# Two message-passing layers on one core: layer two's sums on three column groups of TensorE, and a second fetcher of rows

## The chip, the core and the metric

The kernel runs on one core of a Trainium2 chip. A core has five engines with queues of their own: TensorE (PE, matrix products; its weight loads are shown as PEld), VectorE (DVE), ScalarE (ACT), GpSimd (POOL) and SyncE (SP). SP, ScalarE and POOL also issue transfers (DMAs). The metric is the time of the whole program on the device in microseconds; less is better.

## What is computed

A graph has 6250 nodes and 200,000 edges. A node has 160 features: 64 scalars and 32 vectors of three components. Each edge has a source `src`, a destination `dst` (sorted), four attributes `sh` (one scalar `e0`, one vector `e1`) and ten more, `ea`. Both layers have the same shape: gather the source's row, make a message of it with the edge's attributes, sum the messages by destination, and multiply the sums by small matrices. After each layer comes a residual and a layer norm.

```python
# layer one
m = concat(out0(ss, e0, dot(vv, e1)), out1(ss, vv, e0, e1))     # linear in the source's row
m_agg = segment_sum(m, dst)
x = layernorm(x + (x + relu(linear(m_agg))))
# layer two
w0, w1, w2, w3 = split(relu(ea @ W_fc1) @ W_fc2)                # 64, 64, 32, 32 per edge
y0, y1 = l0[src], l1[src]                                       # linear maps of x, gathered
m0 = w0 * y0 * e0;   m1 = (w1 * y0) * e1;   m2 = (w2 * e0) * y1;   m3 = w3 * dot(y1, e1)
s0..s3 = segment_sums of m0..m3 by dst
x = layernorm(x + self_linear(x) + 0.5 * linear(s0, s3, s1, s2))
```

## The kernel before

**Chunks and tiles.** The edges are cut into 391 chunks of 512. A chunk is four tiles (`J = 4`) of 128 edges, one edge in each partition. Since `dst` is sorted, all edges of a chunk fall into one window of at most 32 neighbouring nodes (or, in the 79 chunks from `HALF = 312` on, into two windows, one for each half of the partitions; there are 470 windows). `ORDER` interleaves these two kinds of chunks: eight of the first kind, then now and then four of the second.

**A chunk's way.** The 128 source rows of a tile are gathered by POOL with an indirect DMA (`gathered`, L244 to L247), from `x` in layer one and from the table `ytab`, which layer one writes, in layer two. The gathered tile `g` comes from a ring of `GRING = 8` chunks. VectorE builds a one-hot matrix of destinations in the window and multiplies it with the four attributes (`onehot`, L453 to L463): `S` has, for each of four tiles, 4 x 32 = 128 columns, 32 for each attribute. In layer two `hidden` (L465, TensorE and ScalarE) and `message` (L477, TensorE's `pw`, VectorE) make the edge's weights and from them the message `m`, two times 160 values for an edge: the first 160 go with attribute 0, the second 160 with attributes 1 to 3.

**The sums.** `matmuls` (L496) multiplies `S` with `g` (layer one) or `m` (layer two), over the four tiles of a chunk, into a PSUM tile `ab` for each window. The rows of `ab` are the 4 x 32 columns of `S`. In layer two one product has 320 columns, and of its 128 x 320 result only two parts are of use: rows 0 to 31 of the first 160 columns, and rows 32 to 127 of the second 160. `joined` (L508, ScalarE) copies the first part over the rows 0 to 31 of the second, so that one block of 128 x 160 is left. `add` (L513) transposes it in blocks of 32 x 32 on VectorE into the free end of `ab`, and adds it to `acc`, which holds the sums of all nodes. When all edges of 128 nodes are done, the parts listed in L650 to L656 project the sums, add the residual and do the norm. A `fp32` product leaves two records in the trace, each of all its columns.

**Two queues help POOL.** Of every 16 chunks SP fetches the last tile of one (place 15), and in layer one ScalarE does so for another (place 7), row by row with the row number from a register: `fetch_rows` (L380). In each of the 16 chunks ahead, the helper loads eight numbers into registers (L396) and issues eight transfers of 640 B (L400). The numbers themselves come by a transfer on SP's queue (`numbers`, L376), ordered halfway through the 16 chunks before, into one of two buffers. `place_rows` (L402) copies the 128 fetched rows into the ring on ScalarE.

**The order of work.** It is written out by hand in L657 to L669: for each step `t` every stage is issued for the chunk `t` less its lag (L649 for layer two: fetching and loading 0, one-hot and hidden 1, message 2, products 3, copy and addition 4). Each engine works through its own share of this list in order. POOL carries only the gathers.

Of the kernel before, what the change touches and what calls it, by code (L numbers as in the profile page):

```python
# [10 lines left out]
F32 = mybir.dt.float32  # L11
BF16 = mybir.dt.bfloat16
I32 = mybir.dt.int32
AF = mybir.ActivationFunctionType
# [4 lines left out]
P = 128  # L19
N = 6250  # L20
E = 200000
D = 160
M0, M1 = 64, 32
J = 4
CH = P * J
NCH = -(-E // CH)
# [12 lines left out]
W = 32  # L39
# [9 lines left out]


EVERY = 16
ROWS = P // EVERY
FOLD = 104


# [29 lines left out]

ORDER = interleaved()
POS = {c: i for i, c in enumerate(ORDER)}
# [165 lines left out]
def windowed(ctx: ExitStack, tc: tile.TileContext, x, srcs, src, rel, low, ident, iota, early, ahead, ea, sh, avec,  # L253
# [6 lines left out]
    nc = tc.nc  # L260
# [94 lines left out]
    def sums(layer, table, gp, hp):  # L355
        with ExitStack() as s:
# [5 lines left out]
            rp = s.enter_context(tc.tile_pool(name=f"r{layer}", bufs=2))  # L362
            pa = s.enter_context(tc.tile_pool(name=f"pa{layer}", bufs=3 if layer else 4, space=PSUM))
# [4 lines left out]
            G, S, SH, ET, H, M, PA, AT, RAW, NUM, ROW = ({} for _ in range(11))  # L368


            helpers = {EVERY - 1: (nc.sync, mybir.EngineType.SP)}
            if not layer:
                helpers[EVERY // 2 - 1] = (nc.scalar, mybir.EngineType.Activation)
            helped = {ORDER[i] for i in range(EVERY // 2, NCH) if i % EVERY in helpers}

            def numbers(c):  # L376
                NUM[c] = rp.tile([1, P], I32, name=f"num{POS[c] % EVERY}")
                nc.sync.dma_start(NUM[c], src[:, c, J - 1:J].rearrange("p a -> a p"))

            def fetch_rows(c):  # L380
                i = POS[c]
                for place, (queue, engine) in helpers.items():

                    k = (i - place - 1) % EVERY
                    due = i - k + EVERY - 1
                    if due >= NCH or ORDER[due] not in helped:
                        continue
                    d = ORDER[due]
                    if d not in NUM:
                        numbers(d)  # L390
                    if d not in ROW:
                        ROW[d] = rp.tile([P, D], F32, name=f"row{place}")
                    if k == EVERY // 2 and due + EVERY < NCH:
                        numbers(ORDER[due + EVERY])
                    a = k * ROWS
                    _, at = nc.values_load_multi_w_load_instructions(  # L396
                        NUM[d][0:1, a:a + ROWS], engines=[engine], min_val=0, max_val=N - 1,
                        skip_runtime_bounds_check_because="node numbers")
                    for n in range(ROWS):
                        queue.dma_start(ROW[d][a + n:a + n + 1, :], table[ds(at[n], 1), :])  # L400

            def place_rows(c):  # L402
                if c in helped:
# [92 lines left out]
            def matmuls(c):  # L496
                one = S.pop(c)
                t = M.pop(c) if layer else G[c]
                n = t.shape[2]
                h = P // len(windows(c))  # L500
                PA[c] = [pa.tile([P, n + D], F32, name="ab") for w in windows(c)]
                for j in range(J):
                    for i, ab in enumerate(PA[c]):
                        nc.tensor.matmul(ab[:, :n], one[h * i:h * i + h, j, :, :], t[h * i:h * i + h, j, :],  # L504
                                         start=(j == 0), stop=(j == J - 1), skip_group_check=True)
                del G[c]

            def joined(c):  # L508

                for ab in PA[c]:  # L510
                    nc.scalar.activation(ab[0:32, D:2 * D], ab[0:32, 0:D], AF.Copy)  # L511

            def add(c):  # L513
                for w, ab in zip(windows(c), PA.pop(c)):
                    if w % 8 == 0:
                        n = min(8, NWIN - w)
                        _, AT[w // 8] = nc.values_load_multi_w_load_instructions(
                            low[0:1, w:w + n], engines=[mybir.EngineType.DVE], min_val=0, max_val=N,
                            skip_runtime_bounds_check_because="clamped on chip")

                    n = D * (layer + 1)
                    tr = ab[:, n:].rearrange("p (b f) -> p b f", f=W)
                    blocks = ab[:, :n].rearrange("p (l b f) -> p l b f", b=5, f=32)
# [38 lines left out]
            def normed(name, b):  # L562
                r = rows(b)
                rs = np_.tile([P, 1], F32, name="rs")
                nc.vector.reciprocal(rs[:r], T.pop(("sd", b))[:r])
                o = T[name, b] = T.pop(("z", b))
                nc.vector.tensor_scalar(o[:r], o[:r], T.pop(("mv", b))[:r, 0:1], rs[:r],
                                        op0=ALU.subtract, op1=ALU.mult)
# [494 lines left out]
```

## Time and profile before

| | |
|---|---|
| median of 3 runs | 5906.23 us (5887.63 to 5917.96) |
| the profiled execution | 3964.1 us, of which the span is 3962.0 |
| mean granted clock of TensorE in it | 0.773 |
| POOL busy | 2900.8 us (73%), gathers of layer one 1428.3, of layer two 1460.6 |
| TensorE busy | 3157.5 us (80%); products `ab` of layer two 977.7, `pw` 662.3 |
| VectorE busy | 2009.5 us (51%) |
| ScalarE busy | 494.3 us (12%) |
| DMA engines | mean 75 GB/s; the 16 engines are busy 20 to 30% |
| row fetches | 3072 by SP in each layer, 2944 by ScalarE in layer one |

The profile shows one execution. Layer one fills its first 1930 us, layer two the rest. "Busy" leaves out the time that an engine spends on issuing transfers and on waiting. In the lines of groups the columns are: line, engine, operation, out<-in and count; then busy us and mean ns of one; then idle us of the engine just before, with what ended most of it. In the waits: who waited for whom, us in all, times, longest. In the timeline: start, duration, engine, line, operation, count. The profiled execution is a good deal shorter than the timed runs.

### The profile page before, as it was taken

To read this page: it belongs to the slowest core of one execution; us is meant where nothing else is said; L and a number is where in the kernel's file an instruction comes from. 1 tells how busy PE (TensorE), PEld (TensorE's weight loads), DVE (VectorE), ACT (ScalarE), POOL (GpSimd) and SP (SyncE) were. 2 spreads that over 40 slices of the span, in tenths; PEclk is the share of its full clock that TensorE was granted. 3 is DMA by queue.
4 is the path that set the end of the run, shared out by engine and by line. 5 is a ranking of instruction groups with operands and counts; after the bars stand their busy time and mean duration, and the time that the engine had idled before them with its cause. 6 is when DMAs were issued, how large, how long until landed. Compare 5 with 4: busy or idle time off the path is not lost.

```text
span 3962.0 us, 71344 instructions
## 1 busy us (share of the span) xinstructions
PE 3157.5 (80%) x12754; PEld 2196.2 (55%) x12755; DVE 2009.5 (51%) x6485; ACT 494.3 (12%) x1288; POOL 2900.8 (73%) x3062
## 2 busy tenths in 40 slices
PE   3346677777777777766799899999999999999998
PEld 3334444444554444544566566666666666666666
DVE  4223323333333334344466666666666666666666
ACT  2000000000000000001111111111111111111111
POOL 6777777777777777777677777777777777666763
PEclk7656655555556566666799999999999899898999
DMA  3322233333333333333232323233333332222321
GB/s 82 74 69 73 73 76 74 75 75 80 75 78 76 79 77 81 77 81 81 71 77 73 76 73 77 75 77 76 78 79 75 78 79 73 70 74 71 76 70 49
DMA packets 223655, 297.53 MB, mean 75 GB/s; under 512 B 77638, under 2 KB 166988, under 8 KB 223194
## 3 DMA queue, kind: packets, MB, share of 16 engines
q0 software_dynamic: 146736, 250.63, 25.6%
q1 hardware_dynamic: 63382, 35.55, 3.4%
q10 hardware_dynamic: 13076, 6.70, 0.6%
q14 instruction: 354, 2.90, 0.2%
q8 instruction: 107, 1.75, 0.2%
HBM read 280.61 MB, written 12.00 MB: 74 GB/s over the span
## 4 chain that ended last, share of the span: by engine, by line
PE 31%; issue 16%; DMA 16%; POOL 14%; SPq 13%; DVE 5%; ACTq 4%; ACT 1%; DVEq 0%; POOLq 0%
PE ab L504 15%; POOL g L247 14%; SPq L400 9%; PE pw L484 8%; DMA g<-in_x,srcs 7%; PE ph L471 4%; ACTq L400 3%; SPq L396 3%; DMA g<-ytab,srcs 3%; DMA row<-in_x 2%; DVE m L492 2%; PE ph L548 1%; DMA early<-in_ea 1%; PE bank L635 1%; ACTq L396 1%
## 5 line engine op out<-in xcount | busy, mean ns | idle before, releaser
L247 POOL DMA_INDIRECT g<-ytab,srcs x1540 | 1460.6, 948 | 541.3 <-issue 408.3
L247 POOL DMA_INDIRECT g<-in_x,srcs x1505 | 1428.3, 949 | 463.6 <-issue 401.9
L504 PE MATMUL ab<-g,S 128*128 128x160 f32 (+1 forms) x3736 | 1038.9, 463 | 552.9 <-DMA g<-in_x,srcs 300.2
L504 PEld LDWEIGHTS ab<-g,S 128*128 128x128 f32 (+1 forms) x3736 | 696.4, 278 | 902.6 <-DMA g<-in_x,srcs 498.1
L504 PE MATMUL ab<-m,S 128*128 128x320 f32 (+1 forms) x3760 | 977.7, 456 | 2.2 <-DVE acc L529 2.0
L504 PEld LDWEIGHTS ab<-m,S 128*128 128x128 f32 (+1 forms) x3760 | 632.7, 201 | 222.8 <-issue 56.0
L484 PEld LDWEIGHTS pw<-fc,h 100*128 100x128 f32 x3128 | 552.5, 203 | 252.5 <-issue 153.0
L484 PE MATMUL pw<-fc,h 100*128 100x192 f32 x3128 | 662.3, 356 | 27.0 <-DVE bank L458 16.2
L462 DVE TENSOR_TENSOR S<-bank,sh 128x384 f32<-128x384 f32 (+2 forms) x782 | 431.2, 551 | 197.2 <-PE ab L504 164.7
L487 DVE TENSOR_TENSOR m<-pw,g 128x256 f32<-128x256 f32 x782 | 328.1, 420 | 373.3 <-PE pw L484 251.0
L527 DVE STREAM_TRANSPOSE ab<-ab 128x160 f32<-128x160 f32 x470 | 169.5, 361 | 677.2 <-PE ab L504 673.1
L492 DVE TENSOR_TENSOR m<-g,pw 128x192 f32<-128x192 f32 x1564 | 474.7, 344 | 0.0
L529 DVE TENSOR_TENSOR acc<-acc,ab 128x120 f32 (+2 forms) x940 | 261.4, 278 | 210.4 <-ACT acc L585 144.0
L474 ACT ACTIVATE h<-ph 100x512 f32<-100x512 f32 x391 | 228.3, 584 | 377.4 <-PE ph L471 377.4
L511 ACT ACTIVATE ab<-ab 32x160 f32<-32x160 f32 x470 | 119.7, 264 | 1208.9 <-PE ab L504 1042.4
L458 DVE TENSOR_TENSOR bank<-ramp,rel 128x96 f32<-128x96 f32 (+2 forms) x782 | 199.7, 255 | 88.2 <-PE bank L635 86.4
L471 PE MATMUL ph<-early,fc 10*100 10x512 f32 x392 | 135.9, 707 | 77.1 <-DMA early<-in_ea 77.1
L525 DVE STREAM_TRANSPOSE ab<-ab 128x160 f32<-128x160 f32 x470 | 167.3, 356 | 20.9 <-ACT ab L511 11.8
L471 PE MATMUL ph<-w_or_et,fc 10*100 10x512 f32 x390 | 128.3, 665 | 57.2 <-DMA w_or_et<-in_ea 57.1
L622 DVE SCALAR_TENSOR_TENSOR base<-pl,a_sb,z 128x160 f32<-128x160 f32 (+1 forms) x49 | 18.8, 384 | 265.7 <-ACT y L619 260.5
L548 PE MATMUL ph<-w_or_et,acc 128*128 128x160 f32 (+1 forms) x490 | 126.7, 436 | 3.5 <-DVE acc L529 2.2
L548 PEld LDWEIGHTS ph<-w_or_et,acc 128*128 128x128 f32 (+1 forms) x490 | 118.7, 304 | 13.2 <-issue 6.7
(95 smaller groups left out, 847.8 us busy)
## 6 DMA issues: line engine op xcount, KB each, us to landing
row<-in_x SPq DMA_DIRECT2D x3072, 0.6 KB
row<-ytab SPq DMA_DIRECT2D x3072, 0.6 KB
row<-in_x ACTq DMA_DIRECT2D x2944, 0.6 KB
g<-ytab,srcs POOLq DMA_INDIRECT x1540
g<-in_x,srcs POOLq DMA_INDIRECT x1505
raw<-in_sh SPq DMA_DIRECT2D x88, 64.0 KB
early<-in_ea SPq DMA_DIRECT2D x98, 40.0 KB
xt<-in_x SPq DMA_DIRECT2D x48, 80.0 KB
```

The source lines that it names most:

```text
L247: nc.gpsimd.indirect_dma_start(out=g[:, j, :], out_offset=None, in_=table, in_offset=bass.IndirectOffsetOnAxis(ap=srcs[:, c, j:j + 1], axi ...
L400: queue.dma_start(ROW[d][a + n:a + n + 1, :], table[ds(at[n], 1), :])
L458: nc.vector.tensor_tensor(oh[:, :, :w], iota[:, None, :w].to_broadcast([P, J, w]), rel[:, c, :, None].to_broadcast([P, J, w]), op=ALU.is_e ...
L462: nc.vector.tensor_tensor(S[c][:, :, :, :w], oh[:, :, None, :w].to_broadcast([P, J, 4, w]), attr[:, :, :, None].to_broadcast([P, J, 4, w]) ...
L471: nc.tensor.matmul(ph[:, i, :], fc1[g:g + 10, :], ET[c // 4][g:g + 10, c % 4 // 2, :], start=True, stop=True)
L474: nc.scalar.activation(H[c], H["p"][:, c % 2, :].rearrange("f (p j) -> f j p", j=J), AF.Relu, scale=FC_SCALE)
L484: nc.tensor.matmul(pw[:, j, :], h[:, q + j, :], fc2, start=True, stop=True)
L487: nc.vector.tensor_tensor(mq[:, :, :, 0:64], pw[:, :, 0:128].rearrange("p j (a u) -> p j a u", a=2), y[:, :, None, 0:64].to_broadcast([P, ...
L492: nc.vector.tensor_tensor(mq[:, :, a, 64:160].rearrange("p j (d u) -> p j d u", d=3), y1, pw[:, :, None, w:w + 32].to_broadcast([P, 2, 3, ...
L504: nc.tensor.matmul(ab[:, :n], one[h * i:h * i + h, j, :, :], t[h * i:h * i + h, j, :], start=(j == 0), stop=(j == J - 1), skip_group_check ...
L529: nc.vector.tensor_tensor(v, v, tr[:, :, :width(c)], op=ALU.add)
L548: nc.tensor.matmul(po[:r], lhs, weights[:, g, :], start=(g == 0), stop=(g == 4))
```

## The change

In layer two `matmuls` now issues three products of 160 columns for each tile and window in place of one of 320: attribute 0 with the first 160 columns of `m` (PSUM partitions 0 to 31), attribute 1 with the second 160 (32 to 63), attributes 2 and 3 with the second 160 (64 to 127). Each product uses a column group of the array of its own (32, 32 and 64 columns). The results lie where `add` wants them, `joined` goes, and the tile `ab` shrinks from 480 to 320 columns.

ScalarE becomes a helper in layer two as well, at place 7 of every 32 chunks: four rows in each of 32 chunks, eleven tiles in all (POOL then has 1529 gathers in layer two, where it had 1540). In both layers and for both helpers the numbers have one buffer now in place of two, and they are ordered when the helper has read the last of the numbers before, in the last of its 16 (or 32) chunks, one chunk ahead of their use.

```diff
-            helpers = {EVERY - 1: (nc.sync, mybir.EngineType.SP)}
-            if not layer:
-                helpers[EVERY // 2 - 1] = (nc.scalar, mybir.EngineType.Activation)
-            helped = {ORDER[i] for i in range(EVERY // 2, NCH) if i % EVERY in helpers}
+            helpers = {EVERY - 1: (nc.sync, mybir.EngineType.SP, EVERY),
+                       EVERY // 2 - 1: (nc.scalar, mybir.EngineType.Activation, EVERY * (layer + 1))}
+            helped = {ORDER[i] for place, (_, _, every) in helpers.items() for i in range(every - 1, NCH)
+                      if i % every == place}
 
-            def numbers(c):
-                NUM[c] = rp.tile([1, P], I32, name=f"num{POS[c] % EVERY}")
+            def numbers(c, place):
+                NUM[c] = rp.tile([1, P], I32, name=f"num{place}", bufs=1)
                 nc.sync.dma_start(NUM[c], src[:, c, J - 1:J].rearrange("p a -> a p"))
...
-                    if k == EVERY // 2 and due + EVERY < NCH:
-                        numbers(ORDER[due + EVERY])
-                    a = k * ROWS
+                    n = P // every
+                    a = k * n
                     _, at = nc.values_load_multi_w_load_instructions(
-                        NUM[d][0:1, a:a + ROWS], engines=[engine], min_val=0, max_val=N - 1,
+                        NUM[d][0:1, a:a + n], engines=[engine], min_val=0, max_val=N - 1,
                         skip_runtime_bounds_check_because="node numbers")
-                    for n in range(ROWS):
-                        queue.dma_start(ROW[d][a + n:a + n + 1, :], table[ds(at[n], 1), :])
+                    if k == every - 1 and due + every < NCH:
+                        numbers(ORDER[due + every], place)
+                    for m in range(n):
+                        queue.dma_start(ROW[d][a + m:a + m + 1, :], table[ds(at[m], 1), :])
...
             def matmuls(c):
                 one = S.pop(c)
                 t = M.pop(c) if layer else G[c]
-                n = t.shape[2]
                 h = P // len(windows(c))
-                PA[c] = [pa.tile([P, n + D], F32, name="ab") for w in windows(c)]
+
+                sides = ((0, 1, 0), (1, 2, D), (2, 4, D)) if layer else ((0, 4, 0),)
+                PA[c] = [pa.tile([P, 2 * D], F32, name="ab") for w in windows(c)]
                 for j in range(J):
-                    for i, ab in enumerate(PA[c]):
-                        nc.tensor.matmul(ab[:, :n], one[h * i:h * i + h, j, :, :], t[h * i:h * i + h, j, :],
-                                         start=(j == 0), stop=(j == J - 1), skip_group_check=True)
+                    for a, b, n in sides:
+                        for i, ab in enumerate(PA[c]):
+                            p = slice(h * i, h * i + h)
+                            nc.tensor.matmul(ab[W * a:W * b, :D], one[p, j, a:b, :], t[p, j, n:n + D],
+                                             start=(j == 0), stop=(j == J - 1), skip_group_check=True)
                 del G[c]
-
-            def joined(c):
-
-                for ab in PA[c]:
-                    nc.scalar.activation(ab[0:32, D:2 * D], ab[0:32, 0:D], AF.Copy)
...
-                    if layer:
-                        nc.vector.transpose(tr, blocks[:, 1])
-                    else:
-                        nc.vector.transpose(tr, blocks[:, 0])
+                    tr = ab[:, D:].rearrange("p (b f) -> p b f", f=W)
+                    nc.vector.transpose(tr, ab[:, :D].rearrange("p (b f) -> p b f", f=32))
...
-                stages = [(fetch_rows, 0), (load, 0), (place_rows, 1), (joined, 4), (onehot, 1), (hidden, 1), (add, 4), (message, 2), (matmuls, 3)]
+                stages = [(fetch_rows, 0), (load, 0), (place_rows, 1), (onehot, 1), (hidden, 1), (add, 4), (message, 2), (matmuls, 3)]
```

More of the change, by code (lines that the diff above doesn't have):

```diff
@@ L51 @@
 EVERY = 16
-ROWS = P // EVERY
 FOLD = 104
@@ L381, in fetch_rows @@
                 i = POS[c]
-                for place, (queue, engine) in helpers.items():
-                    k = (i - place - 1) % EVERY
-                    due = i - k + EVERY - 1
+                for place, (queue, engine, every) in helpers.items():
+                    k = (i - place - 1) % every
+                    due = i - k + every - 1
                     if due >= NCH or ORDER[due] not in helped:
@@ L389, in fetch_rows @@
                     if d not in NUM:
-                        numbers(d)
+                        numbers(d, place)
                     if d not in ROW:
                         ROW[d] = rp.tile([P, D], F32, name=f"row{place}")
-                    if k == EVERY // 2 and due + EVERY < NCH:
-                        numbers(ORDER[due + EVERY])
-                    a = k * ROWS
+                    n = P // every
+                    a = k * n
                     _, at = nc.values_load_multi_w_load_instructions(
-                        NUM[d][0:1, a:a + ROWS], engines=[engine], min_val=0, max_val=N - 1,
+                        NUM[d][0:1, a:a + n], engines=[engine], min_val=0, max_val=N - 1,
                         skip_runtime_bounds_check_because="node numbers")
-                    for n in range(ROWS):
-                        queue.dma_start(ROW[d][a + n:a + n + 1, :], table[ds(at[n], 1), :])
+                    if k == every - 1 and due + every < NCH:
+                        numbers(ORDER[due + every], place)
+                    for m in range(n):
+                        queue.dma_start(ROW[d][a + m:a + m + 1, :], table[ds(at[m], 1), :])
             def place_rows(c):
@@ L519, in add @@
                             skip_runtime_bounds_check_because="clamped on chip")
-                    n = D * (layer + 1)
-                    tr = ab[:, n:].rearrange("p (b f) -> p b f", f=W)
-                    blocks = ab[:, :n].rearrange("p (l b f) -> p l b f", b=5, f=32)
-                    if layer:
-                        nc.vector.transpose(tr, blocks[:, 1])
-                    else:
-                        nc.vector.transpose(tr, blocks[:, 0])
+                    tr = ab[:, D:].rearrange("p (b f) -> p b f", f=W)
+                    nc.vector.transpose(tr, ab[:, :D].rearrange("p (b f) -> p b f", f=32))
                     v = acc[:, :, ds(AT[w // 8][w % 8], width(c))]
```

## The prediction

> **What bounds the kernel now.** I read the page's row of slices first, then the groups of each layer by window, the stretches, the waits of the last third of layer two, and last the timeline of TensorE and POOL. First the page:
>
> ```profile
> PE   3346677777777777766799899999999999999998
> POOL 6777777777777777777677777777777777666763
> PEclk7656655555556566666799999999999899898999
> ```
>
> Slices are 99 us. POOL holds one share in both layers, while TensorE is busiest, at nearly full clock, in layer two (from slice 20). What POOL's share means is told by its groups, first in 1932 to 3200 us, then in 3200 to 3900:
>
> ```profile
> L247 POOL DMA_INDIRECT g<-ytab,srcs x1012 | 959.5, 948 | 328.9 <-issue 270.2 <-DMA btab<-base 20.6 <-DVE m L492 14.0
> L247 POOL DMA_INDIRECT g<-ytab,srcs x518 | 491.6, 949 | 208.4 <-issue 135.4 <-DVE bank L458 31.6 <-DVE m L492 24.9
> ```
>
> The first has 1012 gathers in 1268 us, 1.253 us each: 0.948 of work and 0.30 of issue, with nothing between. The second has 518 in 700 us, 1.351 each. At 1.254 they would take 650, so 50 us went to waits for VectorE, that is, for a buffer that compute had not emptied. Layer one (1516 gathers in 1906 us) has 5 us of such waits. The waits of 3200 to 3900 say whom compute waits for:
>
> ```profile
> POOL g L247 <- DVE bank L458: 31.6, 25, 3.7
> PE ph L471 <- DMA w_or_et<-in_ea: 31.2, 12, 3.5
> PE ph L471 <- DMA early<-in_ea: 27.8, 10, 4.2
> ```
>
> TensorE stands 59 us for the edge features that SP's queue brings late, and after such a wait its clock is low for some microseconds. Now TensorE's timeline in a good stretch of layer two (start, duration, name, count):
>
> ```profile
> 3027.28 0.49 PE L484 MATMUL pw<-fc,h 100*128 100x192 f32 x2
> 3027.61 2.32 PE L504 MATMUL ab<-m,S 128*128 128x320 f32 x8
> 3029.86 1.10 PE L471 MATMUL ph<-w_or_et,fc 10*100 10x512 f32 x4
> 3030.89 1.57 PE L484 MATMUL pw<-fc,h 100*128 100x192 f32 x8
> 3032.30 2.32 PE L504 MATMUL ab<-m,S 128*128 128x320 f32 x8
> 3034.45 1.47 PE L484 MATMUL pw<-fc,h 100*128 100x192 f32 x8
> 3035.75 0.43 PE L504 MATMUL ab<-m,S 128*128 128x320 f32 x1
> ```
>
> From 3027.61 to 3035.75 are two chunks: 4.07 us each. The projections add 0.17 (bank group: 490 records over 391 chunks, some 1.4 us per ten). So TensorE wants 4.24 us a chunk at full clock, and POOL 1540 x 1.254 / 391 = 4.94. **POOL is the bound, TensorE is close behind**, and takes over where its clock falls. Last, the ends: POOL's last gather is at 3912.4, the span ends at 3962.0, and TensorE is busy 41 of these 50 us with the chunks it is behind.
>
> The profiled execution took 3964.1 us (span 3962.0 and 2.1 around it). **The three timed runs have a median of 5906.2, which is 1942 more, and no row says where.** TensorE at half clock all through layer two would not do: 2 x 4.24 x 391 = 3316, with layer one's 1932 and the tail 5300. So I carry a difference over twice, as it stands (an added constant) and times 1.49 (everything slower alike), and place the forecast between, nearer the first.
>
> **The change, part by part.** (1) *The product of 320 columns becomes three of 160, on 32, 32 and 64 columns of the array.* A product stands as two records (1248 products, 2496 records). In the timeline a record of 192 columns takes (3035.75 - 3034.45) / 8 = 0.163 us, one of 320 (3034.45 - 3032.30) / 8 = 0.269, which makes 0.83 ns a column and 0.135 us for 160. A chunk has 8 records now, 2.15 us, and 24 after. If the three groups run at once: 8 x 0.135 = 1.08. If one after the other: 24 x 0.135 = 3.24. The trace has no product on neighbouring column groups. It has them on row groups, in the chunks of two windows:
>
> ```profile
> 3017.58 0.49 PE L484 MATMUL pw<-fc,h 100*128 100x192 f32 x2
> 3018.00 2.42 PE L504 MATMUL ab<-m,S 64*128 64x320 f32 x16
> ```
>
> Sixteen records in the time of eight: two row groups run side by side in full. The Trainium skill ("TensorE: Matmul & The Clock Gate", section "Part 3: Packing small matmuls — row/col tiling") gives 2.38 times for three column groups, by which I estimate 8 x 3 x 0.135 / 2.38 = 1.36 us. I take that: 0.79 saved a chunk, 4.24 becomes 3.45. For two-window chunks the same, since the halves still pair (24 pairs).
>
> A rule speaks against it: "TensorEngine Tiling (Array Packing)", section "Tiling Modes", says that a change of the tiling mode, and not merely of the tile, drains the array, and 32 and 64 columns are two modes. The nearest rows are in layer one, at half clock:
>
> ```profile
> 400.46 0.42 PE L598 MATMUL xp<-ident,z 128*128 128x128 f32 x1
> 400.68 0.42 PE L599 MATMUL xp<-ident,z 128*32 128x128 f32 x1
> 400.89 0.74 PE L504 MATMUL ab<-g,S 128*128 128x160 f32 x2
> ```
>
> 128 columns, then 32, then 128 again: 0.22 and 0.21 us apart, no step at the change. A change of row groups does show one: from two pw records to ab it is 0.42 at 3017.58 against 0.33 at 3027.28. By the row the change of columns costs 0. By the rule it costs 2 x 4 x 0.09 = 0.72 a chunk, and the wide group no longer overlaps the narrow ones (4 passes of 0.135 for each j, 2.16 in all, no gain): 4.24 + 0.73 = 4.97, just over POOL's 4.94, some +30 us and more stalls. I go by the row.
>
> A second cost is the number of instructions: 48 loads and products a chunk in place of 16, and 96 where there are two windows. The densest run of them in the trace is ten pairs in 1.64 us at half clock, 0.16 a pair, and that with 79 to 104 columns to load. At 0.16 a pair a chunk would take 3.9, at nothing 1.08. I put no price on it, since the pairs there are held by the columns loaded, and keep it for the range.
>
> (2) *The copy of 32 rows on ScalarE goes* (470 x 0.264 = 120 us of ScalarE, 0.46 of delay before VectorE's transpose where there are two). It lies beside POOL's gathers: nothing, now and after.
>
> (3) *ScalarE fetches one tile in 32 chunks of layer two*: eleven tiles, so 11 gathers x 1.254 = 13.8 us off POOL, on the bound. It pays with 11 x 128 row fetches. One costs 0.30 of its queue in layer one (0.235 and two register steps), four of them 1.2 a chunk, and the load of the numbers up to 0.82. ScalarE is busy 17% of layer two, so 2 us of 4.94 lie in its idle time. Queued behind them on ScalarE are the relu of the next chunk and the square root of the norm, for which TensorE and VectorE wait. TensorE has most of a chunk of slack once (1) holds, and the ring of eight tiles some 20 us. Nothing, then; were that slack gone, 2 us on some chunks.
>
> (4) *The numbers are ordered one chunk ahead, in one buffer, in place of eight chunks and two.* SP must wait until the helper has read the old ones (11 times in layer two, 23 in layer one, ScalarE's place), and behind that stand SP's edge features and rows. The helper then reads them one chunk later. SP is tied to VectorE anyway at each block's output (its wait there is 178 us in 36 times in layer two). Between 0 and 34 x 4.2 us, where 4.2 is the longest wait on a late transfer above. Layer one's POOL passes ScalarE's waits of 466 us for rows with 5 us lost, so I take 0.
>
> **Sum.** Gathers -13.8. Stalls of POOL: 51 becomes some 10, -41 (a less busy TensorE has a lower clock, as layer one's 0.55 to 0.65 shows, so not to nothing). Tail: seven chunks left at 0.79 less, and a smaller lag to begin with: -15 (layer one ends 21.5 after its last gather, so -28 at most, -6 at least). Together -70 of 3964, 3894. On the timed median: 5906 - 70 = 5836, or 5906 - 104 = 5802; forecast **5828**. What stays is 1529 gathers: the large saving on TensorE lies off the path.
>
> **The rivals.** *Column groups run one after the other (ends slower).* Place: every ab product of layer two. 4.24 + 1.09 = 5.33 us a chunk, 391 x 5.33 = 2084 against the 1980 between first and last gather, and with TensorE the bound its waits for edge features (126 us in layer two) count in part: +170 on the profile, 6076 to 6160, say 6100. It decides once a chunk's sums exceed 2.85 (4.94 - 4.24 + 2.15). For: no row shows neighbouring column groups at once; the drain rule and the floor per pair end here too. Against: row groups do it in full. *The gain is eaten.* Drain or pair floor leaves TensorE where it was; only the gathers go: 5906 - 14 to -25, 5885. *The timed runs are held by TensorE*, not by POOL, and 0.79 a chunk counts at half clock: 5906 - 391 x 1.6 = 5280. For: the missing 1942 us. Against: the 5300 above. *The queues bite*: (3) and (4) cost more than the gathers give, at most 34 x 4.2 less 14: between 5935 and 6035, say 5990.
>
> **How the numbers follow.** Forecast case 0.46, its own range 5775 to 5870. One after the other 0.27, gain eaten 0.13, timed runs held by TensorE 0.08, queues 0.06. What a measurement of this kernel can tell from no change is 0.5%, 30 us. Faster 0.46 + 0.08 = 0.54; same 0.13; slower 0.33. Range: at the low end the case at 5280 is left out (0.08) and the scaled gain kept, 5710; at the high end one after the other with the factor 1.49 (170 becomes 253) is kept, 6190, and full drains on top are left out.
>
> **What would show it.** Right: ab records 128x160 on three groups starting within some 10 ns, ab under 1.6 us a chunk, POOL at 75.6% busy in all stretches of layer two, TensorE's clock below 0.9, the last gather near 3860, tail near 35. Wrong: ab over 2.85 us a chunk, starts 0.135 apart, POOL under 73% from the start of layer two; or waits of SP and ScalarE at the numbers of several microseconds with edge features later than now.

## The result, and the profile after

| | before | changed |
|---|---|---|
| median, 4 runs each | 5912.09 us (5887.63 to 5927.44) | 6173.54 us (6151.01 to 6200.72) |
| ratio | | 1.0448, 95% interval 1.0388 to 1.0508 |
| the profiled execution | 3964.1 us | 6151.0 us, span 6149.1 |

The change costs 261 us, 4.5%, where a gain of 78 was forecast. To read the numbers one thing must be known: the chips of these runs are of two kinds, on one of which (chip A below) the kernel before takes 3957 us, and on the others (chips B) 5827 to 5917, so that every ratio here is against runs of before on the same chip. One chip of the runs below is of the first kind, four are of the second. The profile shown of before is like that of chip A (e1 below); the timed runs of the table, and the profile of the changed kernel, are like those of chips B.

The page of the changed kernel, its row of slices (154 us each) and the gathers of the two layers, with the products of layer two between them:

```profile
PE   2222232343333343444578888888888888888988
...
POOL 4444444544444444544444444444444544444442
PEclk7555565665565666666678887888878888888889
...
L246 POOL DMA_INDIRECT g<-ytab,srcs x1529 | 1451.0, 949 | 1646.8 <-DVE bank L458 679.8
L246 POOL DMA_INDIRECT g<-in_x,srcs x1505 | 1427.3, 948 | 1538.6 <-PE ab L507 830.4
L507 PE MATMUL ab<-m,S 128*32 128x160 f32 (+2 forms) x11280 | 1599.9, 354 | 260.6 <-issue 223.6
```

A gather still takes 0.949 us, and TensorE's clock in layer two is 0.7 to 0.8 where it was 0.9. POOL, busy 73% before, is at 47%. Most of that is the kind of chip and not the change: a kernel in which only the order of the numbers is new (e6 below, on a chip B) has POOL at 49% and a mean clock of 0.81 in layer two, where the changed kernel has 0.82. POOL has 1.5 to 1.6 ms of idle time in each layer, and the largest part of it is put down to TensorE in layer one and to VectorE in layer two, that is, to tiles that compute has not emptied. In layer two the wait for VectorE's `bank` (the comparison that makes the one-hot matrix) is 680 us, against 37 in layer two of before and 469 in e6, whose two lines are these:

```profile
POOL g L247 <- DVE bank L458: 37.4, 44, 3.7
```

```profile
POOL g L247 <- DVE bank L461: 468.7, 123, 12.8
```

The sums of layer two take 1600 us in place of the 978 of before. The waits of the changed kernel from 3050 us on, and those of SP's queue, name what compute waits for:

```profile
POOL g L246 <- DVE bank L458: 679.8, 165, 12.7
...
ACT h L474 <- DMA row<-ytab: 403.2, 110, 17.8
...
ACT g L405 <- DMA row<-ytab: 111.0, 20, 11.4
```

```profile
SPq L400 <- DMA row<-ytab: 254.8, 187, 9.9
```

ScalarE, which should have fetched rows in idle time, holds its relu `h` for 403 us until rows land, and SP's queue stands 255 us at its own row fetches, waiting for rows that are under way. Neither wait was in the profile before, and e6 has 28 us of SP's and none of `h` for rows. (Waits on chips B are to be read with care: many semaphore updates are not in their traces, 2895 of VectorE's 4297 and 2994 of TensorE's 3657 being recorded here against 4773 of 4876 and 3574 of 3632 in e1, so that a wait can be put down to the wrong engine.) Last, TensorE's timeline in a good stretch of layer two:

```profile
5248.61 1.63 PE L628 MATMUL bank<-wc,acc 128*128 128x160 f32 x10
5250.16 1.10 PE L471 MATMUL ph<-w_or_et,fc 10*100 10x512 f32 x4
5251.20 1.57 PE L484 MATMUL pw<-fc,h 100*128 100x192 f32 x8
5252.70 3.32 PE L507 MATMUL ab<-m,S 128*32 128x160 f32 x24
5255.94 1.57 PE L484 MATMUL pw<-fc,h 100*128 100x192 f32 x8
5257.44 1.27 PE L507 MATMUL ab<-m,S 128*32 128x160 f32 x9
5259.11 0.31 PE L507 MATMUL ab<-m,S 128*32 128x160 f32 x1 [0.39 <-issue]
5260.52 1.64 PE L507 MATMUL ab<-m,S 128*64 128x160 f32 x12 [1.10 <-issue]
```

The 24 records of a chunk take 5255.94 - 5252.70 = 3.24 us, while `pw` beside them takes 1.57 as it does at 3030.89 of before, so at the same clock. 3.24 is the price forecast for groups one after the other, not the 1.36 hoped for. And in the last three rows TensorE stops between two products and waits for nothing that the profile shows; the profile of before has no such pause.

### The profile page after: what moved, and what is told of

It reads as the page before. It is cut to its first block, busy times and chain, and to the rows that moved or that the text cites. A ratio compares the mean times of both kernels' runs of the same rounds, so it can differ in the third digit from the quotient of the medians.

```text
span 6149.1 us, 90380 instructions
## 1 busy us (share of the span) xinstructions
PE 3697.8 (60%) x20274; PEld 2235.2 (36%) x20275; DVE 2001.5 (33%) x6485; ACT 395.2 (6%) x829; POOL 2890.3 (47%) x3051
## 5 line engine op out<-in xcount | busy, mean ns | idle before, releaser
L507 PE MATMUL ab<-m,S 128*32 128x160 f32 (+2 forms) x11280 | 1599.9, 354 | 260.6 <-issue 223.6
L507 PE MATMUL ab<-g,S 128*128 128x160 f32 (+1 forms) x3736 | 769.1, 415 | 1156.7 <-ACT g L405 725.3
L507 PEld LDWEIGHTS ab<-m,S 128*32 128x32 f32 (+2 forms) x11280 | 612.1, 126 | 1226.4 <-issue 1212.0
L484 PE MATMUL pw<-fc,h 100*128 100x192 f32 x3128 | 741.5, 388 | 31.4 <-issue 25.6
L484 PEld LDWEIGHTS pw<-fc,h 100*128 100x128 f32 x3128 | 604.5, 223 | 277.0 <-issue 224.1
L605 PE MATMUL pl<-w_or_et,xT 128*128 128x320 f32 (+1 forms) x98 | 65.7, 771 | 472.9 <-ACT xT L598 345.6
L471 PE MATMUL ph<-w_or_et,fc 10*100 10x512 f32 x390 | 147.5, 747 | 95.1 <-DMA w_or_et<-in_ea 93.3
L605 PEld LDWEIGHTS pl<-w_or_et,xT 128*128 128x128 f32 (+1 forms) x98 | 23.8, 298 | 485.4 <-ACT xT L598 353.4
```

The source lines that it names most:

```text
L471: nc.tensor.matmul(ph[:, i, :], fc1[g:g + 10, :], ET[c // 4][g:g + 10, c % 4 // 2, :], start=True, stop=True)
L484: nc.tensor.matmul(pw[:, j, :], h[:, q + j, :], fc2, start=True, stop=True)
L507: nc.tensor.matmul(ab[W * a:W * b, :D], one[p, j, a:b, :], t[p, j, n:n + D], start=(j == 0), stop=(j == J - 1), skip_group_check=True)
```

## The experiments

**Which kind of chip (e1, e5, e12, e16).** The two kernels themselves, unedited. The kernel before, on chip A:

> The kernel before, unchanged, for a second profile of it. The profile shown of it lasts 3964 us, its timed runs 5906. If the timed state is another way of running (SP's and ScalarE's queues in stretches of 0.7 us per instruction, as in the profile after), this profile lasts some 5900 us and shows such stretches, several hundred us of gaps over 0.3 us on SP between its row fetches, where the first one shows 123. If the first profile is the rule, it lasts 3964 again.

3946.5 us, span 3944.4, and the same profile as the one shown: layer one's gathers end at about 1907 us. So the 1942 us that no row of the first profile explained go with the place where the same program runs. Each chip was used in one stretch of time only, so whether it is the chip, its host or the hour isn't shown. The changed kernel, on three chips B:

> The changed kernel, unchanged, on the chip where the kernel before takes some 3960 us. Groups alone cost 161 us there (1.041) and helpers alone 228 us (1.058). If the two causes add up, ratio 1.09 to 1.10. If both only take the same slack (the sums are late either way), 1.06 to 1.07.

> The changed kernel once more. Where before takes 3957 us: the sums alone cost 161 us there and the fetches alone 229 us. If both act through the same slack of TensorE they don't add: 4190 to 4260; if they add, 4345. Where before takes 5840 to 5910: 1.045 times before again.

> The changed kernel once more. Where before takes 3957 us: 4190 to 4260 if its two parts act through the same slack of TensorE, 4345 if they add. Where before takes 5.84 to 5.92 ms: 1.046 times before again.

1.0466 (1.0426 to 1.0505), 1.0467 (1.0422 to 1.0511) and 1.0517 (1.0481 to 1.0553), against before at 5837, 5917 and 5827 us. The changed kernel itself never ran on a chip A.

What differs between the kinds shows in SP's queue in layer one. First before on chip A, then the changed kernel on a chip B, from about the same moment:

```profile
795.77 15.89 SPq L400 DMA_DIRECT2D row<-in_x  x32
```

```profile
795.80 17.22 SPq L400 DMA_DIRECT2D row<-in_x  x22
```

A row, with its share of the loads of numbers, costs the queue 0.50 us in the one and 0.78 in the other. Not every row is dearer: from one row to the next it is 0.41 us in the median of both runs. But in the first 8 us of the second line most of SP's instructions begin 0.70 us after the one before, or twice that, where the first line has steps of 0.06 to 0.31 between the loads; and the register instructions among them have no wait recorded. Such bursts come again and again. The sums of the pauses between two instructions (over 0.38 us each, ahead of an instruction without a recorded wait; from the trace's records, us):

| kernel | SP | ScalarE | TensorE |
|---|---|---|---|
| before, chip A (e1) | 0.5 | 0 | 0 |
| changed, the profile above | 893 | 356 | 218 |
| numbers' order only (e6) | 959 | 309 | 7 |
| fetches and order (e14) | 921 | 303 | 6 |
| three groups only (e13) | 820 | 258 | 155 |
| four equal groups (e8) | 870 | 250 | 436 |
| three products on 128 columns (e17) | 901 | 263 | 258 |
| no row fetches (e9) | 8 | 0 | 22 |
| no row fetches, four groups (e10) | 2 | 0 | 418 |

All but e1 are on chips B. The sums are low: register instructions of some 0.03 us that are recorded with 0.70 themselves come on top (863 us on SP in the changed kernel, none in e1). SP and ScalarE have the pauses with row fetches and not without them; TensorE has next to none with the products of before, and many with more products. VectorE and POOL have 1 and 0 us of them in the changed kernel.

**The three groups alone (e2 on chip A, e13 and e18 on chips B).** The edit of `matmuls`, `joined` and `add`; helpers and numbers as before.

```diff
-                    for i, ab in enumerate(PA[c]):
-                        nc.tensor.matmul(ab[:, :n], one[h * i:h * i + h, j, :, :], t[h * i:h * i + h, j, :],
+                sides = ((0, 1, 0), (1, 2, D), (2, 4, D)) if layer else ((0, 4, 0),)
...
+                    for a, b, n in sides:
+                        for i, ab in enumerate(PA[c]):
+                            p = slice(h * i, h * i + h)
+                            nc.tensor.matmul(ab[W * a:W * b, :D], one[p, j, a:b, :], t[p, j, n:n + D],
```

> Part one of the change alone (three products on 32, 32 and 64 columns, no copy on ScalarE); helpers and numbers as before. Drain theory: a change between 32 and 64 columns drains the array, a chunk's sums take 3.2 us at full clock in place of 2.15, and this alone makes the kernel slower, ratio 1.03 to 1.06 against before. Queue theory: the slowdown comes from ScalarE's fetches and the later numbers, and this kernel is within 1% of before.

> The three column groups alone (the edit of e2). Where before takes 5.84 to 5.92 ms: if the drain between 32 and 64 columns is the cause there too, TensorE again does its sums in 3.3 us a chunk against 2.15, and the time is 120 to 180 us over before (ratio 1.020 to 1.030). If TensorE's stalls with more instructions are the cause, as with the four equal groups (e8, e11), ratio 1.02 too, but with the sums' busy time no longer than before. If the row fetches of SP and ScalarE hold everything there: ratio under 1.01. Where before takes 3957 us: 1.041 again.

> The three column groups alone (the edit of e2 and e13), for the chip of e17. Where before takes 5.84 to 5.92 ms: 1.021 again. Where before takes 3957 us: 1.041 again.

On chip A 4118.3 us against 3957.6, ratio 1.0408 (1.0391 to 1.0425), +161 us. On chips B 1.0213 (1.0183 to 1.0243), +121, and 1.0208 (1.0172 to 1.0244), +129. On chip A the mechanism is plain, since nothing pauses there. TensorE's timeline of e2:

```profile
3006.14 1.47 PE L484 MATMUL pw<-fc,h 100*128 100x192 f32 x8
3007.54 3.32 PE L507 MATMUL ab<-m,S 128*32 128x160 f32 x24
3010.78 1.10 PE L471 MATMUL ph<-early,fc 10*100 10x512 f32 x4
```

The single records at 3007.54 say how 3.24 us come about. In each tile the two groups of 32 columns start 7 ns apart and run side by side; their second pass begins 0.153 later. The group of 64 columns then begins 0.230 later, its second pass 0.186 after that, and the next tile's 32 columns after another 0.229. A pass streams for 0.136. So four passes, 0.54 us, each of them alone, carry 0.09 more at each of the two changes of width and 0.07 more at the second passes: 0.81 us a tile. Chunks of two windows do no better (3.30 us in the median). POOL, in layer two of e2, loses what the forecast thought it would win:

```profile
POOL g L247 <- DVE m L492: 119.6, 85, 4.8
POOL g L247 <- DVE bank L458: 118.8, 164, 3.2
```

In e1 these are 36.5 and 26.3 us:

```profile
L247 POOL DMA_INDIRECT g<-ytab,srcs x1525 | 1443.3, 946 | 502.8 <-issue 400.4 <-DVE m L492 36.5 <-DVE bank L458 26.3
```

TensorE is busy nine tenths and more of every slice of layer two in e2.

**Four equal groups (e4 on chip A, e8 and e11 on chips B).** Attributes 2 and 3 get a group of 32 columns each, so that no width changes. In e4 with the new fetches, in e8 and e11 with those of before.

```diff
-                sides = ((0, 1, 0), (1, 2, D), (2, 4, D)) if layer else ((0, 4, 0),)
+                sides = ((0, 1, 0), (1, 2, D), (2, 3, D), (3, 4, D)) if layer else ((0, 4, 0),)
```

> The changed kernel with four products of 32 columns (attribute 3 split from attribute 2), so that all groups have one width. Drain theory: all four start within some 25 ns, a chunk's sums take 1.1 to 1.4 us at full clock, and the kernel is faster than the changed one by the whole of what the drains cost and below before, ratio 0.93 to 0.98 against before. Queue or instruction-count theory: as slow as the changed kernel or slower (1.04 to 1.08), since it has 2500 more weight loads and as many products.

> Four products of 32 columns, with the helpers and numbers of the kernel before. Drain theory: sums of a chunk take 1.1 to 1.3 us in place of 2.15, POOL is the bound throughout, and the kernel is faster than before by POOL's remaining stalls and part of the tail: 3957 less 40 to 80, ratio 0.980 to 0.990. If the number of instructions cost something by itself (97900 are in the kernel with helpers), 1.00 or more.

> The kernel before with layer two's sums by four equal groups of 32 columns alone (the edit of e8). Where before takes 3957 us: if only the drain between 32 and 64 columns costs time, the four equal groups take 1.3 us a chunk, POOL stays the bound and loses less than 51 us to waits: 3900 to 3957. If the number of TensorE's instructions costs time by itself (96 to 128 more a chunk), as the rival has it, 3990 to 4120. Where before takes 5840 to 5910: 2.3% above before again.

e4 takes 4132.2 us, 1.0447 (1.0424 to 1.0469), and must be held against e3, which has its fetches and the old product: 4186.1. On chip A four groups so gain 54 us where three cost 161 (over the old fetches). Part of the 54 may be ScalarE's copy, which goes with the groups and which in e3 waits behind rows. The timeline of e4, a chunk of one window and one of two:

```profile
3004.69 1.29 PE L507 MATMUL ab<-m,S 128*32 128x160 f32 x32
...
3008.45 1.53 PE L507 MATMUL ab<-m,S 64*32 64x160 f32 x64
```

32 records in the time of eight passes (8 x 0.136 = 1.09, and a lead-in): the four groups start 7 ns apart and run together in full. With more products than the three groups have, they are faster, so on chip A it is the unlike widths that cost, not the number; two groups of 64 columns were not run. The Trainium skill's rule that I had set aside, that a change of the tiling mode and not only of the tile drains the array ("TensorEngine Tiling (Array Packing)", section "Tiling Modes"), agrees with e2 and e4, with 0.09 us at each change; the traces show the late start, not the drain itself.

On chips B it is otherwise: e8 gives 1.0235 (1.0192 to 1.0277) and e11 1.0213 (1.0168 to 1.0259), no better than three groups, though nothing drains. The timeline of e11:

```profile
5007.80 0.29 PE L507 MATMUL ab<-m,S 64*32 64x160 f32 x1 [0.79 <-issue]
5008.53 0.29 PE L507 MATMUL ab<-m,S 64*32 64x160 f32 x1 [0.43 <-issue]
5009.24 0.31 PE L507 MATMUL ab<-m,S 64*32 64x160 f32 x1 [0.42 <-issue]
5009.95 0.42 PE L507 MATMUL ab<-m,S 64*32 64x160 f32 x1 [0.40 <-issue]
```

TensorE starts one product every 0.72 us and waits for nothing recorded: the step of SP's bursts, now on TensorE.

**Three products without groups (e17, chip B, beside e18).** To tell the change of width from the number of products there: the product of 320 columns is cut in three along its columns, all on the full array. As many products as the three groups, no change of width.

```diff
-                        nc.tensor.matmul(ab[:, :n], one[h * i:h * i + h, j, :, :], t[h * i:h * i + h, j, :],
+                    for a, b in ((0, 107), (107, 214), (214, 320)) if layer else ((0, n),):
+                            nc.tensor.matmul(ab[:, a:b], one[h * i:h * i + h, j, :, :], t[h * i:h * i + h, j, a:b],
```

> The kernel before with layer two's product of 320 columns cut into three of 107, 107 and 106 columns, all on the 128 columns of the array: as many products and loads as the three column groups, the same stream as before (2.15 us a chunk at full clock), no group to change. If the drain is what the groups cost: within 0.5% of before on either kind of chip where the loads of 128 columns keep up with products of 0.09 us. If the number of products is what they cost: 1.02 times before where before takes 5.84 to 5.92 ms, with TensorE standing still some 150 us. Where before takes 3957 us, the number costs nothing by itself as far as e4 shows: 3957 to 3990.

Layer two's sums come out wrong in this kernel; it is read for its time alone, its instructions, their sizes and its transfers being as given. 6026.7 us, ratio 1.0186 (1.0150 to 1.0221), beside 1.0208 for the three groups on the same chip. The expectation that the stream stays at 2.15 us was off; the timeline says 2.76:

```profile
5011.57 2.83 PE L505 MATMUL ab<-m,S 128*128 128x107 f32 x24
5014.33 1.10 PE L471 MATMUL ph<-w_or_et,fc 10*100 10x512 f32 x4
```

So e17 has 0.6 us more a chunk (its loads, perhaps; not shown) and 258 us of pauses, the three groups 1.1 more and 170 us, and the four groups 0.9 less and 440 us, and all cost some 2%. What they share is the number of products. On chips B that number by itself is enough for about 2%; how much of the three groups' 2.1% is the change of width there, these runs don't tell.

**The fetches and their order (e3 on chip A, e14 on a chip B).** The edit of `helpers`, `numbers` and `fetch_rows`, with the old product.

```diff
-            helpers = {EVERY - 1: (nc.sync, mybir.EngineType.SP)}
-            if not layer:
-                helpers[EVERY // 2 - 1] = (nc.scalar, mybir.EngineType.Activation)
+            helpers = {EVERY - 1: (nc.sync, mybir.EngineType.SP, EVERY),
+                       EVERY // 2 - 1: (nc.scalar, mybir.EngineType.Activation, EVERY * (layer + 1))}
```

> The helpers' part of the change alone (ScalarE fetches one tile in 32 chunks of layer two, numbers one chunk ahead in one buffer); the product of 320 columns and the copy on ScalarE as before. Queue theory: ratio 1.03 to 1.06 against before. Drain theory: within 1.5% of before, since only eleven gathers go and some waits for numbers come.

> The new fetches and their new order alone (the edit of e3). Where before takes 5.84 to 5.92 ms: if ScalarE's rows in layer two tie up SP's queue as they did where before takes 3957 us, 150 to 250 us over before (ratio 1.025 to 1.04). If the two parts add there, this ratio and that of the groups alone make 1.046 together. If the fetches cost nothing more there, since POOL waits for rows in any case: ratio under 1.01.

Chip A: 4186.1 us, 1.0582 (1.0564 to 1.0599), +229 us, the dearer half of the change. Chip B: 1.0283 (1.0241 to 1.0326), +173 us. The waits of e3 in layer two, and then those of SP's queue:

```profile
DVE m L488 <- PE pw L485: 443.2, 241, 9.8
...
ACT ab L512 <- DMA row<-ytab: 193.5, 68, 8.4
POOL g L247 <- DVE bank L459: 169.0, 93, 6.5
ACT g L406 <- DMA row<-ytab: 152.3, 31, 8.0
PE ph L472 <- DMA w_or_et<-in_ea: 136.0, 46, 7.3
PE ph L472 <- DMA early<-in_ea: 110.0, 38, 6.0
```

```profile
SPq L401 <- DMA row<-ytab: 237.6, 209, 5.4
```

Against e1 on the same chip:

```profile
DVE m L487 <- PE pw L484: 232.5, 165, 7.0
...
PE ph L471 <- DMA early<-in_ea: 66.4, 23, 4.4
...
PE ph L471 <- DMA w_or_et<-in_ea: 54.7, 23, 4.0
...
ACT g L405 <- DMA row<-ytab: 40.6, 12, 5.4
...
POOL g L247 <- DVE bank L458: 26.3, 32, 4.8
```

```profile
SPq L396 <- DMA row<-ytab: 2.1, 5, 0.7
```

ScalarE's issues themselves cost what I had estimated: four rows take 1.66 us of its queue. What was missed is what waits for them. The trace's semaphore records show that the transfers of SP and of ScalarE end on the same eight semaphores, in turn, and that each transfer is issued only after the one before it on its semaphore has landed. In layer two of before only SP uses them. With ScalarE's rows among them SP waits at its own rows (238 us in 209 times; in e1 it waits 2 us in 5 times for rows), its edge features come later (`ph` waits 246 us in place of 121), and TensorE with them. ScalarE's next copy or relu stands behind its own rows (194 us), and TensorE and VectorE behind that: in e3 `pw` is waited for 443 us by VectorE's `m`, 232 in e1, and POOL waits 169 us for `bank` in place of 26. e14 shows the same lines on a chip B (`ab` of ScalarE 182 us, SP's rows 142).

**Only the numbers' order (e6), and fewer rows (e7), both beside e5 on one chip B.** e6 has the new order, ScalarE's place in layer two taken out; in e7 ScalarE fetches one row a chunk (one tile in 128 chunks) in place of four. Both have the old product. The line of e7 against that of the changed kernel:

```diff
-                       EVERY // 2 - 1: (nc.scalar, mybir.EngineType.Activation, EVERY * (layer + 1))}
+                       EVERY // 2 - 1: (nc.scalar, mybir.EngineType.Activation, EVERY * (7 * layer + 1))}
```

> Of the helpers' part only the order of the numbers (one chunk ahead, one buffer); no fetches by ScalarE in layer two; product of 320 columns. Numbers theory: the wait for ScalarE at the numbers is what makes the helpers' part slow, and this kernel has most of its 1.058. Coupling theory: ScalarE's fetches in layer two make it slow, and this kernel is within 0.7% of before.

> The helpers' part with ScalarE fetching one row a chunk in layer two in place of four (one tile in 128 chunks); product of 320 columns. Coupling theory: SP's and ScalarE's transfers share eight completion semaphores, each transfer waits for the one before it on its semaphore, and one transfer a chunk is enough to tie SP to ScalarE, and the relu of each chunk to the landing of a row: at least half of the 5.8% stays, 1.03 to 1.06. Issue theory: ScalarE's time for registers and issues (2 us a chunk with four rows, some 0.9 with one) is what costs: 1.00 to 1.02.

e6 1.0055 (1.0037 to 1.0072), +32 us; e7 1.0121 (1.0076 to 1.0167). The order costs little, one row a chunk about 0.7% more, and four rows (e14, on another chip) 2.3% over e6. e7 was to part the tie by semaphores, which one row a chunk might be enough to make, from ScalarE's own time for issues, which would fall to less than half. It doesn't: some 30% of the cost stays with a quarter of the rows, and the waits go with the rows as well (SP's for rows 28, 68 and 142 us in e6, e7 and e14, the wait of ScalarE's `ab` for rows none, 40 and 182). That compute waits for rows is shown; how the cost divides between the semaphores and ScalarE's queue is open. The gathers of e5 and e6 place the loss: layer one's take 2969 us in e5 (the whole change) and 2966 in e6, layer two's 3002 and 2789. All that the change costs beyond the order is in layer two.

**Do the parts add?** e13, e14 and e16 ran on one chip: +121, +173, and +292 for both. They add to within 2 us (each time is uncertain by some 20), though both act through the same chain of TensorE, VectorE and POOL.

**No row fetches at all (e9, e10, e15, chips B).** If SP and ScalarE pause where they fetch rows, the fetches may cost more than the gathers they replace. POOL gathers all tiles in e9 and e15; e10 has the four groups as well.

```diff
-            helped = {ORDER[i] for i in range(EVERY // 2, NCH) if i % EVERY in helpers}
+            helped = set()
```

> The kernel before without any row fetch by SP or ScalarE, in both layers: POOL gathers all 1564 tiles of each layer. It has 72 gathers more than the kernel before, 72 x 1.254 = 90 us. Where before takes 3957 us: 4047, and the numbers that SP and ScalarE no longer fetch must not show in POOL's stalls. Where before takes 5840 to 5910: theory A (the row fetches are what those chips do badly; SP and ScalarE fall behind with them, and POOL waits for tiles whose rows come late): 4050 to 4500, well under before. Theory B (those chips stall SP and ScalarE after any instruction, whatever it is): 5800 to 6000, since edge features, norms and relus stay on the two engines.

> The kernel before without any row fetch by SP or ScalarE, once more. Where before takes 5.84 to 5.92 ms: 0.82 times before again. Where before takes 3957 us: 72 gathers more on POOL, 72 x 1.254 = 90 us, 4047; less than 4030 if SP's and ScalarE's fetches cost POOL waits there too.

> As e9, and layer two's sums by four products of 32 columns, without ScalarE's copy of 32 rows. Where before takes 3957 us: POOL is the bound and TensorE has 0.8 us a chunk more to spare, so e9's time less up to 40 us, 4010 to 4047; above e9 only if the number of TensorE's instructions costs something by itself. Where before takes 5840 to 5910: theory A as e9, within 1%; theory B 5700 to 6000.

e9 takes 4876.2 us, 0.8247 (0.8213 to 0.8282) times before, and e15 4827.1, 0.8288 (0.8266 to 0.8310): 71 gathers more, and 1000 to 1041 us less. e10 takes 5205.4, 0.8801 (0.8760 to 0.8841), 329 us more than e9 on the same chip, for 418 us of TensorE's pauses. Gathers of e9, from its page:

```profile
L247 POOL DMA_INDIRECT g<-ytab,srcs x1564 | 1483.9, 949 | 1089.0 <-issue 424.7
L247 POOL DMA_INDIRECT g<-in_x,srcs x1552 | 1473.6, 950 | 754.4 <-issue 426.9
```

Layer one's idle time falls by half (1539 us in the changed kernel). e9 beats both kernels on chips B. On chip A it wasn't run; there the 71 gathers at 1.254 us should make it 89 us slower than before, an estimate. What still holds it at some 4850 us on chips B, against that estimate of 4047 and over the 4500 allowed for, is open.

## Why the prediction was wrong

The forecast was 5828 us, faster; the kernel takes 6173.5. That this lies within the stated 5710 to 6190 is luck: the high end was kept for groups one after the other alone, and more than half of the loss is the fetches. (That end is also 31 us more than the 5906 + 253 that it was made from.)

- *What bounds the kernel* held on chip A: POOL, its gathers at 1.254 us, with TensorE close behind in layer two. On chips B POOL is busy less than half of the time in the changed kernel and in e6. On chip A +161 us came as soon as TensorE's sums passed the 2.85 us a chunk given as the point of decision.
- *The step that failed first is (1), "by the row the change of columns costs 0 ... I go by the row".* The row was rightly read, since its steps of 0.21 us are no more than 128 columns take at half clock. But it is of transposes with nothing beside them, and whether their 32 columns are a change of mode at all the traces don't say; in e2, where groups of 32 and 64 columns take turns, each change costs 0.09. The 1.36 us failed with it: the 2.38 times of the Trainium skill ("TensorE: Matmul & The Clock Gate", section "Part 3: Packing small matmuls — row/col tiling") is for three groups of 32 columns each, and was taken over to 32, 32 and 64. The rule's side of the step was the better one, its 0.09 taken from a change of row groups, and still too low: 2.16 + 0.72 = 2.88 us a chunk, measured 3.24, since the second passes too are 0.02 to 0.05 late. The rival "one after the other" had 3.24 by two errors that cancel, leaving out both the side by side of the narrow groups and the lateness at the changes; its time on the profile, +170, met e2's +161.
- *The second cost of (1), the number of products, "I put no price on it",* is right on chip A, where 64 pairs of a load and a record of a two-window chunk run in 3009.91 - 3008.45 = 1.46 us (e4), and wrong on the chips that were timed: e17, e8 and e11 cost 1.9 to 2.35% without any change of width.
- *The step that failed as badly, and on the timed chips cost more, is (3), "nothing, then".* The 2 us on ScalarE were well sized. That they lie in idle time was read from its busy share alone; the price is 229 us on chip A and 173 on a chip B (with the order), through SP's queue and through ScalarE's own next instruction (the groups: 161 and 121 to 129). The 11 gathers were taken away as said, worth 13.8.
- *(4)*, 0 of a bound of 143 us: measured 32. *(2)*, the copy at nothing: not separately shown; it goes in every kernel with groups. (470 x 0.264 is 124 us, not 120, which changes nothing.)
- *Sum.* POOL's stalls in layer two were to fall from 51 us to 10; in e2 they rise from some 40 to 200 us, and in e5 they are some 1090 against some 860 in e6.
- *The carried offset of 1942 us* came from the place of the run and there from the row fetches in large part (e9 is 1000 us below before), so that an added constant and a factor were both without ground. It also put the timed runs where the number of products has a price. The rival that laid it on TensorE is out: more than half of it, some 1060 us, is lost in layer one, where TensorE is busy 2 to 4 tenths.
- *The signs given* for the wrong case came for the most part: `ab` over 2.85 us a chunk; POOL at 73, 68 and 66% in the three stretches of layer two in e2 (its 47% in the changed kernel says nothing, being the same in layer one); edge features later than before in e3, behind rows and not, as named, behind the numbers.
- *The rivals.* Two of them came together, groups one after the other and queues that bite, each of which I had priced alone; the sum of the two parts, measured on one chip B, is the measured change there.

## What to carry to other kernels

Cut a product into column groups of one width: groups of 32 and 64 columns in turn don't run together, four equal groups do, though on chips like B the added products cost 2% by themselves. A row that is to price a change of mode must show that change between products such as will run. Before a queue gets more transfers, look up which semaphores they end on and what is next on the engine that issues them, since an engine that is busy 17% of layer two can still be one whose every microsecond of delay is handed on. And where a profile is a third shorter than the timed runs, find out first whether it was taken where they ran.

## What the hardware showed that I had not expected

- Four groups of 32 columns run wholly side by side: 32 records of 160 columns in 1.29 us (e4), 8 passes of 0.136 and a lead-in, where the estimate from the 2.38 times of three groups would have given 1.83 (8 x 4 x 0.136 / 2.38).
- SP's and ScalarE's transfers end on eight semaphores in common, so that one queue's rows hold up the other's (238 us in e3, 2 in e1).
- On some chips SP, ScalarE and TensorE begin their instructions only every 0.70 us or more, in bursts: pauses of 893, 356 and 218 us in the changed kernel, 0.5, 0 and 0 for before on chip A. POOL's gathers and the length of a product are the same on both. That supplying the instructions is what lags there is a guess and not shown; the transfers that the profile calls `instruction` take about as long on both (medians near 1.0 and 0.4 us on their two queues).
- The row fetches, made to take load off POOL, cost 1000 us on these chips (e9, e15).
